# Graph attention's f column: 32-node blocks turned on VectorE and spread through DRAM instead of TensorE transposes

## The chip, the core and the metric

The kernel runs on one NeuronCore of a Trainium2 chip. The engines of a core work in parallel, each through its own list of instructions in order: TensorE (PE) does matmuls and transposes through the matmul array, VectorE (DVE) and ScalarE (ACT) do elementwise work, GpSimd (POOL) small side work, and SyncE (SP) issues the DMAs. PE writes into PSUM, which is eight banks here; everything else lives in SBUF, and inputs and outputs in DRAM. Engines wait for each other by semaphores. The metric is the device time of one launch in microseconds; the median of three runs before the change is 3039.1 us (3038.93 to 3040.48).

## What is computed

There are 64 graphs of 256 nodes with 256 features, and an adjacency matrix each. A graph passes four layers, each with a residual and a layer norm: multi-head attention with a feed-forward block, two graph attentions, and a relational convolution of two steps. The change concerns the two graph attentions. Cut to the core:

```python
Wh = einsum('bnd,de->bne', h, W)
f_i = Wh @ a1                                # one number per node
f_j = Wh @ a2
e = f_i[:, :, None] + f_j[:, None, :]        # 256 x 256 scores of a graph
e = leaky_relu(e, 0.2)
e = where(adj > 0, e, -inf)
alpha = softmax(e, axis=-1)
out = einsum('bij,bjd->bid', alpha, Wh)
```

The score of a pair of nodes is a sum of two numbers, one per node. In a tile with the key nodes on the partitions and the query nodes along the free dimension, one of the two (g) is a column that an instruction can add per partition; the other (f) must lie along the free dimension, the same row of 256 numbers on all 128 partitions. But the product that makes h leaves f as a column, one number per partition. Something has to turn it and spread it over the partitions.

## The kernel before

Graphs are handled one by one as sets of operations, and a planner in the kernel (`Plan`, lines 51 to 202) orders the operations of all 64 graphs together. Each operation has an engine, a cost in microseconds written beside it, the tiles that it reads and writes, and a due time that follows from the graph's number (46 us a graph). `schedule` plays the engines in time by these costs: each engine takes the ready operation with the earliest due time whose buffers are free. A result is seen by another engine a lag later (`LAG`, line 58; 3.5 us for SP), by the same engine at once (line 192). Buffers come from rings of fixed size (`RINGS`, line 25), eight PSUM banks among them. PE's three ways of tiling the array ("full", "row", "col") are kept together, and a change between them is given a cost (`SWITCH`). What comes out is one fixed order of instructions for each engine, including SP's DMAs; on the chip each engine follows its order and waits only for semaphores. At any time operations of about three graphs are mixed.

A graph attention is `gat` (lines 767 to 804). Its steps:

- the features are transposed on PE and evicted by ACT (`transposed`, L596 and L599);
- two products of 128 nodes each with the weights, widened by two columns for f and g (`product`, L605, "gw");
- eviction to the tile h, by ACT for layer 2 (L776), by DVE with a bias for layer 1 (L778);
- the spread of f: for each half of the nodes, one transpose on PE of the f column repeated over 128 columns. The result, f along the free dimension on every partition, is in a PSUM bank (L787);
- two score instructions on DVE, f + g, limited by the mask gm (L792), the leaky ReLU on DVE (L795), exp on ACT (L797);
- two products of e with h on PE (L605, "h,e"), which include the softmax sum through a column of ones, then reciprocal, scaling and residual on DVE, and the layer norm.

SP issues for each graph the loads of x, adj, xr (x once more) and adj again, each 256 KB, and the store of the result (L579, L902).

After the main path a check on sums decides whether a general, slow version is run as well; with these inputs it is not. It uses two constants, `eye` and `ones_b`, which are made at the kernel's start.

The lines around the change:

Of the kernel before, what the change touches and what calls it, by code (L numbers as in the profile page):

```python
# [25 lines left out]
         "xr": 2, "hid": 1, "h": 3, "e": 4, "n": 2, "rel": 3, "hi": 2, "lo": 2, "o": 4}  # L26
# [24 lines left out]
class Plan:  # L51
# [6 lines left out]
    LAG = {"PE": 0.21, "DVE": 0.13, "ACT": 0.13, "POOL": 0.08, "SP": 3.5}  # L58
    TO = {"PE": 0.06, "POOL": 0.05}
    SWITCH = 0.2  # L60
# [145 lines left out]
def tile_gnn_stack(ctx: ExitStack, tc: tile.TileContext, t: dict, out: bass.AP):  # L206
# [114 lines left out]
    ones_b = filled([P, P], BF16, "ones_b", 1.0)  # L321
    ones = filled([P, HD], F32, "ones", 1.0)
    neghalf = filled([P, NT], F32, "neghalf", -0.5)
    eye = filled([P, N // P, N], BF16, "eye", 0.0)
    for h in range(N // P):
        nc.vector.tensor_copy(eye[:, h, h * P : (h + 1) * P], ident_b)
# [153 lines left out]
    def main_path(plan):  # L480
# [11 lines left out]
        plan.ring("bank", 8, bank)  # L492

# [61 lines left out]
        def graph(g):  # L555
# [14 lines left out]

            def new(ring, shape, dtype=F32):
                return plan.tile(ring, shape, dtype)
# [16 lines left out]
            def transposed(xt):  # L589
# [9 lines left out]
                act(0.48, lambda: nc.scalar.copy(xT(), pt()), [pt], [xT])  # L599
# [7 lines left out]
            def layer_norm(y):  # L607
# [21 lines left out]
                dve(1.0, stats, [y], [mv, stat])  # L629
# [27 lines left out]
            def projections(xT):  # L657
# [22 lines left out]
                act(0.49, lambda: nc.scalar.copy(v(), pv()), [pv], [v])  # L680
                return qk, v

            def attention(xT, am):
# [6 lines left out]
                for kt in range(NB):  # L690
# [11 lines left out]
                    pe("row", 1.08, scores, [qk], s, [p[kt, r] for r in range(4)])  # L702
                    for r in range(4):
                        pr, k = p[kt, r], 8 * g + 4 * kt + r
                        act(0.61, lambda pr=pr, k=k, sr=s[r]: nc.scalar.activation(  # L705
# [8 lines left out]
                for hg in range(KB):  # L714
# [12 lines left out]
                    pe("col", 1.31, values, [v] + both + list(p.values()), [pc], [ctxT, inv])  # L727
                    dve(1.67, lambda hg=hg, pc=pc: nc.vector.reciprocal(inv()[:, hg, :], pc()[:, 1, :]), [pc], [(inv, hg)])  # L728
                    dve(0.34, lambda hg=hg, pc=pc: nc.vector.tensor_tensor(
                        ctxT()[:, hg, :], pc()[:, 0, :], inv()[:, hg, :], op=ALU.mult), [pc, (inv, hg)], [(ctxT, hg)])  # L730
                act(0.61, lambda: nc.scalar.activation(inv(), inv(), AF.Identity, accum_out=seen_inv[:, g : g + 1]), [inv], [inv])
                return ctxT

            def product_plus(lhs, reads, rhs, n, add):
# [5 lines left out]
                dve(0.66, lambda: nc.vector.tensor_tensor(y(), po(), add(), op=ALU.add), [po, add], [y])  # L740
# [26 lines left out]
            def gat(xt, layer, gm, seen, bias, finish):  # L767
# [3 lines left out]
                for i in range(NB):  # L771
# [3 lines left out]
                    if bias is None:  # L775
                        act(0.29, lambda i=i, ph=ph: nc.scalar.copy(h()[:, i, 0 : D + 2], ph()), [ph], [(h, i)])  # L776
                    else:
                        dve(0.34, lambda i=i, ph=ph: nc.vector.tensor_tensor(h()[:, i, 0 : D + 2], ph(), bias, op=ALU.add),  # L778
                            [ph], [(h, i)])
# [3 lines left out]
                pf = new("bank", [P, N])  # L783

                def spread():
                    for i in range(NB):
                        nc.tensor.transpose(pf()[:, i * P : (i + 1) * P],  # L787
                                            h()[:, i, F_COL : F_COL + 1].to_broadcast([P, P]), ident)

                pe("full", 0.22, spread, [(h, 0), (h, 1)], [pf], [e])  # L790
                for i in range(NB):
                    dve(0.40, lambda i=i: nc.vector.scalar_tensor_tensor(e()[:, i, :], pf(), h()[:, i, G_COL : G_COL + 1],  # L792
                                                                         gm()[:, i, :], op0=ALU.add, op1=ALU.min),
                        [pf, (h, i), gm], [(e, i)])
# [3 lines left out]
                for i in range(NB):  # L798
# [3 lines left out]
                    dve(0.12, lambda po=po, r=r: nc.vector.reciprocal(r(), po()[:, ONE : ONE + 1]), [po], [r])  # L802
# [13 lines left out]
            def layer2(xt, gm):  # L816
                def finish(i, z, po, r):
# [5 lines left out]
                    dve(0.37, lambda: nc.vector.scalar_tensor_tensor(n(), n(), 1.0, xt()[:, i, :], op0=ALU.min,  # L823
                                                                     op1=ALU.add), [n, xt], [n], "uses")
                    dve(0.37, lambda: nc.vector.scalar_tensor_tensor(zi(), n(), -1.0, zi(), op0=ALU.add, op1=ALU.max),
# [16 lines left out]
            def conv(h, layer, rel, rdeg):  # L842
# [18 lines left out]
                for j in range(NB):  # L861
# [8 lines left out]
                    pe("full", 0.46, gather, [rel, hi, lo], [pa])  # L870
# [288 lines left out]
```

## Time and profile before

| what | us |
|---|---|
| median of three runs | 3039.1 |
| time of the profiled execution | 3041.5 |
| its span, first to last instruction | 3039.6 |
| PE busy | 2949.0 (97%) |
| PE weight loads busy | 2257.9 (74%) |
| DVE busy | 2560.6 (84%) |
| ACT busy | 1574.8 (52%) |
| POOL busy | 761.8 (25%) |
| DMA queue of SP | 89.15 MB, 9.9% of 16 engines |

The span runs from the first to the last instruction of one profiled execution; its own time lies 1.9 us above the span and 2.4 us above the median. Busy time counts when an engine works on an instruction. Matmuls overlap, so the time that a matmul occupies PE is the distance to the next one's start and not its shown length. "Idle before" names how long an engine stood just before instructions of a group and what ended it. The mean granted clock of PE is 0.994 of full speed.

### The profile page before, as it was taken

The numbers are of one execution on the slowest core, as the hardware profiler recorded it, in microseconds if no ns is written. First come the engines' busy times: TensorE is split into PE (matmuls) and PEld (weight loads), VectorE is DVE, ScalarE is ACT, GpSimd is POOL, SyncE is SP. The second block draws the span as 40 slices with busy tenths as digits, with TensorE's granted clock in tenths as the row PEclk, the third lists the DMA queues.
The fourth block names the chain that finished last, engine by engine and source line by source line (L and its number), as shares of the span: only waits on it lengthen the run. The fifth ranks groups of instructions, "written<-read, shape, count | busy, mean of one in ns | idle before, by whom it ended". The sixth has DMA issues, their size and how long they took to land.

```text
span 3039.6 us, 49429 instructions
## 1 busy us (share of the span) xinstructions
PE 2949.0 (97%) x17462; PEld 2257.9 (74%) x17462; DVE 2560.6 (84%) x6368; ACT 1574.8 (52%) x3777; POOL 761.8 (25%) x1877
## 2 busy tenths in 40 slices
PE   8999999999999999999999999999999999999897
PEld 6777767777777777777777777777777777777584
DVE  6889798888797987988889888979889879897857
ACT  3455445555554554555455455545555545555444
POOL 2222222222222222222232222222222223222121
PEclk9999999999999999999999999999999999999999
DMA  5001011111010010010110101100101110001000
GB/s 155 25 22 36 19 34 32 29 28 32 22 32 29 29 36 28 25 32 28 29 32 25 36 22 32 32 29 28 30 27 29 29 31 29 28 25 29 8 11 15
DMA packets 91947, 93.56 MB, mean 31 GB/s; under 512 B 5648, under 2 KB 90896, under 8 KB 91696
## 3 DMA queue, kind: packets, MB, share of 16 engines
q1 hardware_dynamic: 91072, 89.15, 9.9%
q8 instruction: 141, 2.31, 0.3%
q0 software_dynamic: 624, 1.19, 0.2%
q14 instruction: 110, 0.90, 0.1%
HBM read 73.54 MB, written 16.78 MB: 30 GB/s over the span
## 4 chain that ended last, share of the span: by engine, by line
PE 71%; DVE 19%; ACT 4%; POOL 3%; issue 2%; SPq 1%; DMA 0%; POOLq 0%; ACTq 0%; DVEq 0%
PE bank L605 57%; PE bank L596 4%; PE bank L724 3%; PE bank L867 3%; DVE p L707 2%; PE bank L699 2%; PE bank L719 2%; DVE st L614 2%; ACT X L626 1%; POOL rstd L620 1%; ACT p L705 1%; DVE o L877 1%; DVE inv L728 1%; DVE both L711 1%; DVE X L740 1%
## 5 line engine op out<-in xcount | busy, mean ns | idle before, releaser
L619 POOL TENSOR_SCALAR rstd<-mv 128x2 f32<-128x2 f32 x384 | 134.0, 349 | 1535.2 <-DVE mv L616 1388.5
L605 PE MATMUL bank<-T,w 128*128 128x256 f32 x2048 | 480.7, 381 | 2.0 <-ACT T L599 1.4
L605 PE MATMUL bank<-cw,T 128*128 128x512 f32 x1024 | 469.7, 601 | 11.3 <-ACT T L599 8.8
L626 ACT ACTIVATE X<-X,rstd 128x256 f32<-128x256 f32 x640 | 349.8, 596 | 236.8 <-POOL rstd L622 151.2
L605 PE MATMUL bank<-w,hid 128*128 128x256 f32 x2048 | 463.3, 380 | 0.0
L605 PEld LDWEIGHTS bank<-w,hid 128*128 128x128 f32 x2048 | 383.5, 190 | 58.6 <-issue 5.1
L605 PEld LDWEIGHTS bank<-T,w 128*128 128x128 f32 x2048 | 376.6, 190 | 58.2 <-issue 5.1
L707 DVE TENSOR_TENSOR p<-p,am 128x512 f32<-128x512 f32 x512 | 329.0, 683 | 31.6 <-ACT p L705 30.2
L605 PEld LDWEIGHTS bank<-cw,T 128*128 128x128 f32 x1024 | 192.0, 192 | 212.6 <-issue 186.2
L705 ACT ACTIVATE p<-bank 128x512 f32<-128x512 f32 x512 | 300.7, 599 | 46.7 <-PE bank L699 45.9
L620 POOL TENSOR_TENSOR rstd<-rstd,neghalf 128x2 f32<-128x2 f32 x384 | 311.2, 810 | 32.0
L599 ACT COPY T<-bank 128x512 f32<-128x512 f32 x384 | 222.0, 586 | 184.8 <-PE bank L596 181.2
L605 PE MATMUL bank<-h,e 128*128 128x259 f32 x1024 | 251.3, 386 | 9.5 <-ACT e L797 7.1
L605 PE MATMUL bank<-T,wqkv 128*128 128x256 f32 x1024 | 247.4, 384 | 6.6 <-ACT T L599 6.6
L757 ACT ACTIVATE hid<-bank,col_b 128x256 f32<-128x256 f32 x512 | 212.1, 472 | 74.8 <-PE bank L605 72.7
L605 PE MATMUL bank<-gw,T 128*128 128x258 f32 x1024 | 247.1, 382 | 1.3 <-ACT T L599 1.2
L614 DVE BATCH_NORM_STATS2 st<-X 128x6 f32<-128x256 f32 x640 | 239.2, 416 | 5.1
L605 PEld LDWEIGHTS bank<-h,e 128*128 128x128 f32 x1024 | 190.7, 190 | 67.4 <-issue 28.0
L728 DVE RECIPROCAL inv<-bank 128x256 f32<-128x256 f32 x128 | 215.3, 1721 | 8.7 <-PE bank L724 8.7
L605 PEld LDWEIGHTS bank<-T,wqkv 128*128 128x128 f32 x1024 | 188.8, 191 | 37.4 <-ACT T L599 9.8
L605 PEld LDWEIGHTS bank<-gw,T 128*128 128x128 f32 x1024 | 190.0, 190 | 32.1 <-ACT T L599 3.2
L781 POOL TENSOR_TENSOR seen_fg<-h 128x4 f32<-128x4 f32 x128 | 54.8, 428 | 624.0 <-DVE h L778 322.7
(124 smaller groups left out, 4966.6 us busy)
## 6 DMA issues: line engine op xcount, KB each, us to landing
adj<-in_adj_dram SPq DMA_DIRECT2D x128, 256.0 KB, 2.8
x<-in_x_dram SPq DMA_DIRECT2D x64, 256.0 KB, 2.8
xr<-in_x_dram SPq DMA_DIRECT2D x64, 256.0 KB, 2.8
out_dram<-o SPq DMA_DIRECT2D x64, 256.0 KB, 2.1
w<-in_W1T_dram SPq DMA_DIRECT2D x1, 1024.0 KB, 12.2
w<-in_W2T_dram SPq DMA_DIRECT2D x1, 1024.0 KB, 19.0
wqkv<-in_WqkvT_dram SPq DMA_DIRECT2D x1, 768.0 KB, 4.7
cw<-in_w_root_dram SPq DMA_DIRECT2D x2, 256.0 KB, 5.5
```

The costliest lines, as they stand in the source:

```text
L596: nc.tensor.transpose(pt()[:, kb, i * P : (i + 1) * P], xt()[:, i, kb * P : (kb + 1) * P], ident)
L599: act(0.48, lambda: nc.scalar.copy(xT(), pt()), [pt], [xT])
L605: nc.tensor.matmul(dst, lhsT=lhs(c), rhs=rhs(c), start=(c == 0), stop=(c == n - 1))
L614: nc.vector.bn_stats(stat()[:, i, :], y()[:, i, :])
L619: nc.gpsimd.tensor_scalar(rstd()[:, 0, :], mv()[:, :, 1], 1.0, EPS, op0=ALU.mult, op1=ALU.add)
L620: nc.gpsimd.tensor_tensor(rstd()[:, 0, :], rstd()[:, 0, :], neghalf[:, 0:NB], op=ALU.pow)
L626: nc.scalar.activation(y()[:, i, :], y()[:, i, :], AF.Identity, bias=rstd()[:, 1, i : i + 1], scale=rstd()[:, 0, i : i + 1])
L705: act(0.61, lambda pr=pr, k=k, sr=s[r]: nc.scalar.activation(pr(), sr(), AF.Exp, accum_out=seen_sum[:, k : k + 1]), [s[r]], [pr])
L707: dve(0.60, lambda pr=pr, kt=kt: nc.vector.tensor_tensor(pr(), pr(), am()[:, kt, None, :].to_broadcast([P, KB, N]), op=ALU.mult), [pr, am] ...
L724: nc.tensor.matmul(pc()[32 * r : 32 * r + 32, 0, :], lhsT=v()[:, kt, HD * h : HD * (h + 1)], rhs=p[kt, r]()[:, hg, :], start=(kt == 0), st ...
L728: dve(1.67, lambda hg=hg, pc=pc: nc.vector.reciprocal(inv()[:, hg, :], pc()[:, 1, :]), [pc], [(inv, hg)])
L757: act(0.36, lambda f=f, k=k, ph=ph: nc.scalar.activation(hid()[:, f + k, :], ph()[:, k, :], AF.Relu, bias=b1[:, f + k : f + k + 1]), [ph, ...
```

## The change

The two PE transposes of each graph attention go. In their place DVE transposes f in blocks of 32 by 32: the f column, repeated 32 times, is turned so that the 32 partitions of a block each hold the block's 32 numbers. SP stores the four blocks of each half into a DRAM tile of 32 rows by 256, so that each of the 32 rows has all 256 numbers, and then loads the 32 rows four times over onto 128 partitions. The scores read f from SBUF instead of PSUM. New rings hold the turned blocks (`own`), the DRAM tile (`f_row`) and the loaded f (`f`), two of each.

`eye` and `ones_b` move into the general version. Some costs and lags that the planner reckons with are changed, so that it orders the work anew.

```diff
-    LAG = {"PE": 0.21, "DVE": 0.13, "ACT": 0.13, "POOL": 0.08, "SP": 3.5}
+    LAG = {"PE": 0.21, "DVE": 0.13, "ACT": 0.13, "POOL": 0.08, "SP": 3.2}
...
-    SWITCH = 0.2
+    SWITCH = 0.1
...
+            def sp(cost, issue, reads, writes):
+                op("SP", cost, issue, reads, writes)
...
-                pf = new("bank", [P, N])
-
-                def spread():
+                own, rows, pf = new("own", [P, NB * 32]), new("f_row", [32, N]), new("f", [P, N])
+
+                def turn():
                     for i in range(NB):
-                        nc.tensor.transpose(pf()[:, i * P : (i + 1) * P],
-                                            h()[:, i, F_COL : F_COL + 1].to_broadcast([P, P]), ident)
-
-                pe("full", 0.22, spread, [(h, 0), (h, 1)], [pf], [e])
+                        nc.vector.transpose(own()[:, i * 32 : (i + 1) * 32], h()[:, i, F_COL : F_COL + 1].to_broadcast([P, 32]))
+
+                dve(0.2, turn, [(h, 0), (h, 1)], [own], "uses")
                 for i in range(NB):
-                    dve(0.40, lambda i=i: nc.vector.scalar_tensor_tensor(e()[:, i, :], pf(), h()[:, i, G_COL : G_COL + 1],
-                                                                         gm()[:, i, :], op0=ALU.add, op1=ALU.min),
-                        [pf, (h, i), gm], [(e, i)])
+                    sp(0.42, lambda i=i: nc.sync.dma_start(rows()[:, i * P : (i + 1) * P].rearrange("r (b n) -> b r n", b=4),
+                                                           own()[:, i * 32 : (i + 1) * 32]), [own], [(rows, i)])
+                sp(0.42, lambda: nc.sync.dma_start(pf(), rows()[None, :, :].to_broadcast([4, 32, N])), [rows], [pf])
+                for i in range(NB):
+                    dve(0.35, lambda i=i: nc.vector.scalar_tensor_tensor(
+                        e()[:, i, :], pf(), h()[:, i, G_COL : G_COL + 1], gm()[:, i, :], op0=ALU.add, op1=ALU.min), [pf, (h, i), gm], [(e, i)], "uses")
...
-                    dve(0.12, lambda po=po, r=r: nc.vector.reciprocal(r(), po()[:, ONE : ONE + 1]), [po], [r])
+                    dve(0.08, lambda po=po, r=r: nc.vector.reciprocal(r(), po()[:, ONE : ONE + 1]), [po], [r])
```

About fifteen other cost figures change by a few hundredths up to 0.12, most of them downwards.

## The prediction

> **What bounds the kernel now.** I read the page's busy table first, then the busy time by stretch, then what TensorE (PE) waited for, then the timeline around the transposes, last the costs by group and the DMA lines.
>
> ```profile
> PE 2949.0 (97%) x17462; PEld 2257.9 (74%) x17462; DVE 2560.6 (84%) x6368; ACT 1574.8 (52%) x3777; POOL 761.8 (25%) x1877
> ```
>
> ```profile
> 1262.00:1540.00 278.00, 274.12 (x1637) 210.60 (x1634) 238.79 (x592) 146.27 (x352) 73.63 (x174) 1.00 0.10 28
> 1540.00:2800.00 1260.00, 1240.57 (x7352) 954.88 (x7352) 1082.72 (x2685) 667.27 (x1602) 329.10 (x792) 1.00 0.10 30
> 2800.00:2980.00 180.00, 162.81 (x929) 123.41 (x928) 132.36 (x332) 82.31 (x191) 33.98 (x110) 0.97 0.03 8
> 2980.00:3040.00 60.00, 41.92 (x162) 23.66 (x160) 42.26 (x132) 23.25 (x49) 9.61 (x31) 0.88 0.06 19
> ```
>
> After stretch and length come PE, PE's weight loads, DVE, ACT and POOL, then the granted clock. PE is busy 98.5% from 1262 to 2800 us and has holes only in the last 240 us, where three graphs drain. DVE, at 86%, is next. PE's waits, in total, times, longest:
>
> ```profile
> PE bank L605 <- ACT T L599: 18.0, 28, 1.1
> PE bank L596 <- ACT X L626: 8.6, 23, 1.7
> PE bank L605 <- ACT e L797: 7.1, 10, 2.4
> PE bank L787 <- DVE h L778: 1.5, 4, 0.8
> ```
>
> The list adds up to some 75 us, start and end included. So the kernel is bound by PE's instruction stream, and a wait put into that stream is paid in full. The attention scores e cost PE only 7.1 us of waiting. The timeline of one spread:
>
> ```profile
> 1288.20 1.03 PE L605 MATMUL bank<-T,w 128*128 128x256 f32 x4
> 1289.06 0.38 PE L787 MATMUL bank<-ident,h 128*128 128x128 f32 x2
> 1289.28 3.60 PE L605 MATMUL bank<-cw,T 128*128 128x512 f32 x8
> 1292.72 0.60 PE L605 MATMUL bank<-h,e 128*128 128x259 f32 x2
> ```
>
> From 1289.06 to the next start, 1289.28, the two transposes hold PE for 0.22 us, although each is shown 0.27 long: matmuls overlap. Costs and transfers (the DMA column is issue to landing):
>
> ```profile
> L787 PE MATMUL bank<-ident,h 128*128 128x128 f32 x256 | 50.6, 276 | 3.4 <-ACT p L705 1.8 <-DVE h L778 1.5
> L792 DVE SCALAR_TENSOR_TENSOR e<-bank,h,gm 128x256 f32<-128x256 f32 x256 | 111.4, 473 | 29.2 <-PE bank L787 29.2
> L823 DVE SCALAR_TENSOR_TENSOR n<-n,X 128x256 f32<-128x256 f32 x128 | 50.3, 414 | 0.0
> L652 DVE TENSOR_TENSOR am<-am,ident_b 128x128 bf16<-128x128 bf16 x128 | 22.9, 221 | 1.6
> L802 DVE RECIPROCAL r<-bank 128x1 f32<-128x1 f32 x256 | 38.7, 157 | 22.5 <-PE bank L605 22.0
> ```
>
> ```profile
> adj<-in_adj_dram SPq DMA_DIRECT2D x128, 256.0 KB, 2.8
> ...
> out_dram<-o SPq DMA_DIRECT2D x64, 256.0 KB, 2.1
> ```
>
> ```profile
> q1 hardware_dynamic: 91072, 89.15, 9.9%
> ```
>
> ```profile
> 1273.42 0.37 SPq L579 DMA_DIRECT2D x<-in_x_dram  x1
> ```
>
> One packet on queue 1 takes 0.099 x 16 x 3039.6 / 91072 = 0.053 us; an issue holds SP 0.37 us.
>
> **The change, part by part.** There are 64 graphs with two graph attentions each: 128 spreads.
>
> *Removed from PE.* 256 transposes, by the spacing above 128 x 0.22 = 28.2 us. The busy column's 50.6 is the far bound. I take 28.2, because the next matmul already starts after 0.22. As PE is the bound, this comes off the end, unless something new stops PE.
>
> [...]
>
> *DVE.* It gains 256 transposes of 32 columns: between L802 (157 ns, one column) and L652 (221 ns, 128 columns), nearer the former, say 170: +44 us. The 256 score instructions read f from SBUF instead of PSUM: 473 to 414 (L823, the same operation from SBUF), -15 us. DVE goes to about 2590 us, 85%; PE's 98% still covers that. If DVE's idle time (16%) were used up, each of these 29 us would show.
>
> *Planner's numbers, ones_b and eye.* The order is replanned. Changes of PE's tiling mode in it go from 345 to 352; each costs about 0.09 (0.31 instead of 0.22 before a row or column stretch), so under 1 us. The constants' memsets move out of the start: under 1 us, beside DMAs. The ops' cost figures change no instruction.
>
> *The path of f.* Formerly evict h, 0.22 us of PE, scores. Now: evict h, two transposes, two stores of 16 KB, a wait on SP for both to land, one load of 128 KB, scores. SP's issues rise from 354 to 738: 384 x 0.37 = 142 us, on an engine otherwise idle; but SP is in order, so while it waits for the stores to land (some 2 us, 128 times) the loads and stores of other graphs queue behind it; they have tens of us. In 123 of 128 cases load follows stores directly; in 91 a load of x, xr or adj stands directly before the stores, and if its buffer comes free late, f is late.
>
> Call X the time from the end of the transposes to f being usable. Handovers are 0.1 each. With 256 KB over 16 engines (16 packets each, 0.85 us), a store has 2.1 - 0.85 = 1.25 us without packets and a load 2.8 - 0.85 = 1.95. The trace has no DMA of this shape; the old ones have 128 rows outermost, the new ones' DRAM side has a dimension of 4 outermost.
> - Low end, all 16 engines: stores 0.37 + 1.25 + 8 x 0.053 = 2.0; load 1.95 + 0.42 = 2.4; X = 0.1 + 2.0 + 2.4 + 0.1 = 4.6.
> - High end, four engines, and a 128-byte packet as dear as a 1 KB one: stores 1.25 + 64 x 0.053 = 4.6; load 1.95 + 32 x 0.053 = 3.65; X = 8.5.
> - Taken: four engines, on the assumption that a DMA is cut along its outermost dimension, which is 128 in the old ones and four here; 128-byte packets at 0.015, nearer their share by bytes (0.007) than the full price: stores 1.25 + 64 x 0.015 = 2.2, load 3.65: X = 6.05.
>
> [...]
>
> The planner's own idea is shorter: its code adds SP's lag of 3.2 to other engines only (line 192), so it lets the load issue as soon as the stores are issued: 0.13 + 3 x 0.42 + 3.2 = 4.6 us. It fills just that much. Where X is longer, PE arrives at the product early and stands.
>
> How much stands there? From the last matmul that makes h (L605, gw) to the product with e (L605, h,e) the chain now takes 0.16 (result after its 0.22 spacing) + 0.37 (eviction) + 0.3 (transposes) + X + 0.86 + 0.69 + 0.63 (scores, leaky ReLU, exp, durations of L792, L795, L797) + four handovers 0.4 = 3.4 + X. Against it I put the PE work that lies between the two in the changed order, at the old spacing: 0.433 per 256-column product, 0.86 per 512, 0.11 per transpose, 0.135 per score matmul, 0.11 per column-tiled one. One case: 16 products with hid (6.93) and 4 with ctxT (1.73) make 8.66. The deciles of the 128 windows are 7.8, 8.2, 8.6, 9.0, 9.2, 10.0, 10.2, 10.8, 11.8; in the last eight only 3.9 to 6.6. In the order of before the median is 6.5 and the chain 3.6 (its part from h to the scores is 0.58 by the timeline); this account then gives 2 us of standing, and the profile 7.1. Adding up what the chain exceeds its window by, with windows that overlap counted once:
> chain 8.0: 13 us; 8.6: 27; 9.0: 43; 9.4: 64; 10.0: 101; 11.8: 255. About 15 of the 64 fall in the last eight windows.
>
> With X = 6.05 the chain is 9.4: +64 us. While PE stands, ACT and DVE catch up: of the 45 us or so that PE waits for others between start and end, I take off a quarter, 12.
>
> **Sum**, against the profiled execution (span 3039.6, its time 3041.5, which is 2.4 above the median 3039.1): 3041.5 - 28 + 64 - 12 = 3065; on the median's scale 3063.
>
> **Rivals.**
> 1. *The transfers are quick and hidden: faster.* X = 4.6, chain 8.0: 3041.5 - 28 + 13 - 2.4 = 3024. For it: the planner reckons with this X, and loads of 256 KB land in 2.8. Against: the DRAM side in blocks of 32 by four, and a store that must land first. It decides below X = 5.2 (chain 8.6, 27 us: break-even).
> 2. *DVE, held at the scores, becomes the bound.* DVE is in order; between transposes and scores its new order has 4.6 us of work in the mean. At X = 6 it is held 198 us in all, in 104 of 128 cases. Of its 479 idle us that would leave 250, but what queues behind the scores (masking p, sums for layer norms) then reaches PE late as well. If half of the 198 reaches PE in place of the 64: 3041.5 - 28 + 99 - 2.4 = 3110. For it: 86% busy between 60 and 2800. Against: such lateness mostly falls into the same standing of PE.
> 3. *Gain and standing cancel*: X about 5.2 to 5.4, 3034 to 3045.
>
> **Chances.** Forecast (chain 9.0 to 10: 3041 to 3100) 0.43; rival 1 (3015 to 3032) 0.34; rival 2 (3090 to 3140) 0.15; rival 3 0.08. A measurement of this kernel tells about 0.2%, 6 us, from no change. So faster 0.34, same 0.08, slower 0.58. Range 3019 to 3118: it cuts the fast end of rival 1 and the slow end of rival 2; the high end X = 8.5 (chain 11.9, some 3270) stays out as unlikely. The likeliest case's own range is 3041 to 3100.
>
> **What will show it.** Right: the loads of f land 3.4 to 3.8 us after issue and the stores about 2; PE's wait for e (ACT, L803) rises from 7 to 50 us or more, in some 60 cases; DVE waits for f at L799; PE's busy time falls by 28 us or, by the column, up to 50. Wrong: f landing in about 2.4 and PE's wait for e under 20 us, then the time is near 3024; or DVE's wait at L799 over 150 us with PE standing for T, X and p too, then over 3090. Also wrong if PE's own order has become worse elsewhere, which waits for others than e would tell.

## The result and the profile after

The changed kernel takes 3222.51 us (median of four, 3220.49 to 3228.47) against 3039.79 (3038.93 to 3040.92) for the kernel before: a ratio of 1.0604 with a 95% interval of 1.0586 to 1.0622. It is 183 us slower. The forecast was 3063 with a range of 3019 to 3118: the direction was right, the size was not. The profiled execution took 3220.49, its span is 3218.7, and its mean granted clock is 0.981 (0.994 before).

Busy time and the chain of waits of the changed kernel (the chain's first line by engine, its second by line):

```profile
PE 2993.2 (93%) x17206; PEld 2260.7 (70%) x17206; DVE 2588.0 (80%) x6620; ACT 1577.3 (49%) x3777; POOL 712.6 (22%) x1877
PE 42%; DVE 32%; DMA 16%; issue 4%; ACT 3%; POOL 2%; SPq 0%; POOLq 0%; DVEq 0%; ACTq 0%
PE bank L607 34%; DMA f<-f_row 11%; DMA f_row<-own 5%; DVE p L709 4%; DVE st L616 2%; DVE e L799 2%; PE bank L598 2%; DVE inv L730 2%; DVE o L883 2%; PE bank L726 2%; DVE e L801 2%; PE bank L873 2%; DVE mv L618 1%; DVE X L585 1%; DVE both L713 1%
```

Before, the chain was 71% PE and 0% DMA. Now the two steps through DRAM, the load of f and the stores, are 16% of it, and DVE is 32%. PE has 256 instructions fewer and yet shows 44 us more busy time, a point that comes back below.

The run in stretches, first one row of the kernel before, then the changed kernel (stretch, length, then PE, its weight loads, DVE, ACT, POOL, the granted clock):

```profile
60.00:1262.00 1202.00, 1184.14 (x7089) 907.68 (x7087) 1026.19 (x2542) 634.90 (x1531) 303.28 (x745) 1.00 0.10 29
```

```profile
60.00:1262.00 1202.00, 1139.89 (x6604) 863.38 (x6604) 990.72 (x2533) 608.26 (x1459) 266.09 (x712) 0.99 0.12 34
1262.00:1540.00 278.00, 254.95 (x1459) 192.13 (x1457) 214.84 (x548) 132.78 (x313) 61.19 (x164) 0.97 0.11 32
1540.00:2980.00 1440.00, 1353.64 (x7837) 1022.84 (x7837) 1177.19 (x3008) 716.35 (x1725) 327.67 (x840) 0.99 0.12 34
```

From 60 to 1262 us PE did 7089 matmuls and now does 6604; from 1262 to 1540 us it was busy 274 of 278 us and did 1637, now it is busy 255 and does 1459. The loss is spread over the whole run and is not an effect of the end.

Waits of PE, and below them of DVE (total, times, longest):

```profile
PE bank L607 <- ACT e L803: 54.0, 34, 3.3
PE bank L607 <- issue: 42.7, 34, 3.2
PE bank L598 <- ACT X L628: 31.1, 46, 5.4
PE bank L607 <- ACT T L601: 17.1, 26, 2.8
PE bank L873 <- DVE lo L861: 15.5, 18, 2.6
```

```profile
DVE e L799 <- DMA f<-f_row: 243.6, 116, 6.6
DVE X L742 <- PE bank L607: 129.1, 59, 6.2
DVE lo L861 <- ACT hi L860: 55.8, 53, 4.9
```

PE's wait for e, where the profile names e, is 54.0 us (7.1 before) in 34 cases, close to the 50 us that the forecast gave as its sign. The 42.7 us of "issue", where the profile names no releaser, stand before the same products of h with e. All idle time of PE before these products, in the changed kernel:

```profile
L607 PE MATMUL bank<-h,e 128*128 128x259 f32 x1024 | 275.6, 414 | 108.6 <-ACT e L803 54.0 <-issue 42.7 <-ACT T L601 2.8
```

So PE stands 108.6 us there (9.5 before). And DVE stands 243.6 us for f, and PE also waits longer for X (31.1 us, 8.6 before) and lo (15.5, 2.9 before), though not for T (17.1, 18.0 before). That is for the most part the sign that the prediction gave for its rival 2: DVE held over 150 us, with PE standing for other results too.

One spread in the timeline:

```profile
1515.10 0.30 DVE L791 STREAM_TRANSPOSE own<-h 128x32 f32<-128x32 f32 x2
...
1515.33 1.08 SPq L795 DMA_DIRECT2D f_row<-own  x2
...
1517.87 0.54 SPq L797 DMA_DIRECT2D f<-f_row  x1
...
1522.05 0.91 DVE L799 SCALAR_TENSOR_TENSOR e<-f,h,gm 128x256 f32<-128x256 f32 x2 [0.32 <-DMA f<-f_row]
```

The transposes end at 1515.40, the scores begin at 1522.05, released by the load: X is 6.65 us. Read in this way over all 128 spreads, the median is 6.65 and the mean 6.8 (0.6 from store to store, 2.0 from the second store to the load, 4.06 from the load to the scores).

And what it costs, first DVE, then PE in the same place:

```profile
2417.36 0.33 DVE L791 STREAM_TRANSPOSE own<-h 128x32 f32<-128x32 f32 x2
...
2423.11 0.88 DVE L799 SCALAR_TENSOR_TENSOR e<-f,h,gm 128x256 f32<-128x256 f32 x2 [3.83 <-DMA f<-f_row]
2424.02 0.69 DVE L801 SCALAR_TENSOR_TENSOR e<-e 128x512 f32<-128x512 f32 x1
2428.24 0.88 DVE L799 SCALAR_TENSOR_TENSOR e<-f,h,gm 128x256 f32<-128x256 f32 x2 [3.53 <-DMA f<-f_row]
...
2429.77 0.69 DVE L585 TENSOR_TENSOR X<-X,row_ln_g 128x512 f32<-128x512 f32 x1
```

```profile
2425.48 1.99 PE L607 MATMUL bank<-h,e 128*128 128x259 f32 x8 [1.13 <-issue]
2430.62 3.23 PE L607 MATMUL bank<-h,e 128*128 128x259 f32 x8 [3.15 <-issue]
```

DVE stands 3.8 us for one f and, three instructions later, 3.5 us for the next one; the layer norm's work of L585 and all behind it begin only after both. The second f was turned by 2417.69 and is usable at 2428.24, 10.6 us later: its stores left SP only at 2419.94, because SP stood with the first spread's load until 2419.30.

### The profile page after: what moved, and what is told of

Its sections match the earlier page's. It is cut to its first block, busy times and chain, and to the rows that moved or that the text cites. A ratio compares the mean times of both kernels' runs of the same rounds, so it can differ in the third digit from the quotient of the medians.

```text
span 3218.7 us, 49919 instructions
## 1 busy us (share of the span) xinstructions
PE 2993.2 (93%) x17206; PEld 2260.7 (70%) x17206; DVE 2588.0 (80%) x6620; ACT 1577.3 (49%) x3777; POOL 712.6 (22%) x1877
## 4 chain that ended last, share of the span: by engine, by line
PE 42%; DVE 32%; DMA 16%; issue 4%; ACT 3%; POOL 2%; SPq 0%; POOLq 0%; DVEq 0%; ACTq 0%
PE bank L607 34%; DMA f<-f_row 11%; DMA f_row<-own 5%; DVE p L709 4%; DVE st L616 2%; DVE e L799 2%; PE bank L598 2%; DVE inv L730 2%; DVE o L883 2%; PE bank L726 2%; DVE e L801 2%; PE bank L873 2%; DVE mv L618 1%; DVE X L585 1%; DVE both L713 1%
## 5 line engine op out<-in xcount | busy, mean ns | idle before, releaser
L621 POOL TENSOR_SCALAR rstd<-mv 128x2 f32<-128x2 f32 x384 | 121.6, 317 | 1965.3 <-DVE mv L618 1666.6
L607 PEld LDWEIGHTS bank<-T,w 128*128 128x128 f32 x2048 | 385.0, 192 | 64.7 <-ACT T L601 5.7
L607 PE MATMUL bank<-h,e 128*128 128x259 f32 x1024 | 275.6, 414 | 108.6 <-ACT e L803 54.0
L607 PEld LDWEIGHTS bank<-h,e 128*128 128x128 f32 x1024 | 199.3, 203 | 179.7 <-issue 142.8
L799 DVE SCALAR_TENSOR_TENSOR e<-f,h,gm 128x256 f32<-128x256 f32 x256 | 113.3, 481 | 243.9 <-DMA f<-f_row 243.6
L803 ACT ACTIVATE e<-e 128x512 f32<-128x512 f32 x128 | 80.6, 630 | 297.1 <-DVE e L801 291.3
```

What stands on the lines that cost most here:

```text
L607: nc.tensor.matmul(dst, lhsT=lhs(c), rhs=rhs(c), start=(c == 0), stop=(c == n - 1))
L621: nc.gpsimd.tensor_scalar(rstd()[:, 0, :], mv()[:, :, 1], 1.0, EPS, op0=ALU.mult, op1=ALU.add)
L799: dve(0.35, lambda i=i: nc.vector.scalar_tensor_tensor(e()[:, i, :], pf(), h()[:, i, G_COL : G_COL + 1], gm()[:, i, :], op0=ALU.add, op1=A ...
L803: act(0.52, lambda: nc.scalar.activation(e(), e(), AF.Exp), [e], [e])
```

## The experiments

Times are medians with their lowest and highest. Each experiment is compared with the kernel before on the same chip; the ratio has its 95% interval.

**Which part of the change costs? e1: the changed kernel with PE's spread back.**

```diff
-                own, rows, pf = new("own", [P, NB * 32]), new("f_row", [32, N]), new("f", [P, N])
+                pf = new("bank", [P, N])
...
-                dve(0.2, turn, [(h, 0), (h, 1)], [own], "uses")
+                pe("full", 0.22, spread, [(h, 0), (h, 1)], [pf], [e])
...
-                sp(0.42, lambda: nc.sync.dma_start(pf(), rows()[None, :, :].to_broadcast([4, 32, N])), [rows], [pf])
```

> The changed kernel with the spread of f put back on PE (two transposes into a PSUM bank, scores from the bank); the new cost figures, lags, SWITCH and the moved constants stay. Theory A (the path of f through DRAM costs all the time, the replanned order nothing): within 0.5% of before, 3025 to 3055 us. Rival (the new cost figures give a worse order): 3100 us or more, and then at least 60 of the 183 us belong to them.

Measured: 3045.94 (3042.58 to 3047.56) against 3042.17, ratio 1.0013 (1.0003 to 1.0022). The planner's new figures, the moved constants and the order made from them cost 4 us. The other 179 belong to the change from PE's spread to the path of f.

**e2: the changed kernel with no spread at all; the scores read a constant row.**

```diff
-                own, rows, pf = new("own", [P, NB * 32]), new("f_row", [32, N]), new("f", [P, N])
+                pf = c_f
...
-                dve(0.2, turn, [(h, 0), (h, 1)], [own], "uses")
...
-                sp(0.42, lambda: nc.sync.dma_start(pf(), rows()[None, :, :].to_broadcast([4, 32, N])), [rows], [pf])
```

> The changed kernel without the path of f: no transposes, no stores, no loads; the scores read a constant zero tile in its place, so f is left out of the scores. Theory A (removing 128 pairs of PE transposes is worth their spacing, 0.22 us each): 3039 - 28 = 3011, between 3000 and 3022. Rival (the pairs are worth the busy column, 50 us, or more because a PSUM bank per attention comes free): under 3000. If it is over 3030, the gain was never there.

Measured: 3040.18 (3038.86 to 3043.83) against 3042.17, ratio 0.9995 (0.9986 to 1.0005). Both theories missed; it is the third outcome that was named, over 3030: with the transposes gone and nothing in their place, 6 us are gained against e1, not 28. The removal was therefore tested by itself below (e7, e8, e11, e12).

**e3: PE's spread is used, and the new chain runs beside it unread.**

```diff
-                sp(0.42, lambda: nc.sync.dma_start(pf(), rows()[None, :, :].to_broadcast([4, 32, N])), [rows], [pf])
+                sp(0.42, lambda: nc.sync.dma_start(spare(), rows()[None, :, :].to_broadcast([4, 32, N])), [rows], [spare])
...
+                pe("full", 0.22, spread, [(h, 0), (h, 1)], [pf], [e])
```

> The changed kernel with both: PE spreads f as before and the scores use that; besides, f is turned on DVE, stored and loaded as in the change, and nobody reads it. Theory A (it is the wait for f that costs): 3040 to 3075, since DVE has 51 us more of transposes and SP more to issue but nothing waits. Rival (contention: DVE's extra work, SP's queue held by its waits, DMA traffic): 3130 or more.

Measured: 3049.26 (3046.65 to 3049.99), ratio 1.0023 (1.0013 to 1.0033), 3 us above e1. The 384 DMAs, their packets and DVE's 256 transposes cost almost nothing as work, so contention is not what costs. What is left is the wait for f; e13 takes it away by itself.

**e4: the planner is told what the path takes, X = 6.9 us: 0.6 per store, 1.5 from the stores to the load, 0.55 for the load, 3.5 until it has landed.**

```diff
-    LAG = {"PE": 0.21, "DVE": 0.13, "ACT": 0.13, "POOL": 0.08, "SP": 3.2}
+    LAG = {"PE": 0.21, "DVE": 0.13, "ACT": 0.13, "POOL": 0.08, "SP": 3.5}
+    STORE = 1.5
...
-                    a.ready = max(a.ready, end if a.engine == e else seen + self.TO.get(a.engine, 0.0))
+                    a.ready = max(a.ready, (end + self.STORE if e == "SP" else end) if a.engine == e
+                                  else seen + self.TO.get(a.engine, 0.0))
...
-                    sp(0.42, lambda i=i: nc.sync.dma_start(rows()[:, i * P : (i + 1) * P].rearrange("r (b n) -> b r n", b=4),
+                    sp(0.6, lambda i=i: nc.sync.dma_start(rows()[:, i * P : (i + 1) * P].rearrange("r (b n) -> b r n", b=4),
...
-                sp(0.42, lambda: nc.sync.dma_start(pf(), rows()[None, :, :].to_broadcast([4, 32, N])), [rows], [pf])
+                sp(0.55, lambda: nc.sync.dma_start(pf(), rows()[None, :, :].to_broadcast([4, 32, N])), [rows], [pf])
```

> The changed kernel with the planner told what the trace of the changed kernel shows: a load of f may issue 1.5 us after the stores' issue ends (before: at once), issues cost 0.6 and 0.55, SP's lag 3.5. The median PE work between h and its product with e grows from 9.2 to 11.9 us, DVE's work between transposes and scores from 4.6 to 6.6 us in the mean. Theory A (the path is 2.2 us longer than the planner thought and each engine stands for that): with a chain of 10.2 the account of windows gives 26 us of standing instead of 116; time 3020 to 3070, PE's clock back to 0.99. Rival (the path itself, two DMAs in a row on an in-order SP, is what costs, however it is planned): over 3130.

Measured: 3056.05 (3054.33 to 3061.87), ratio 1.0052 (1.0035 to 1.0068). The same instructions in an order that knows the delay: 166 of the 183 us are back. The path itself had not become shorter: from the first store to the load are 2.6 us as in the changed kernel. X, read up to the scores, is 7.4 us in the median, but DVE stands for f in only 31 of the 128 cases, and in the others X includes time in which f was there and DVE was at other work. DVE's and PE's waits in e4:

```profile
DVE e L801 <- DMA f<-f_row: 49.6, 31, 6.6
```

```profile
PE bank L600 <- ACT X L630: 15.5, 27, 4.6
PE bank L609 <- ACT T L603: 14.7, 22, 2.2
PE bank L609 <- ACT e L805: 9.7, 11, 3.4
```

DVE is held 49.6 us instead of 243.6, PE waits 9.7 for e.

**e5: the planner's figures as in the changed kernel, but quicker DMAs: stores of four rows, and a load with 128 outermost on both sides.**

```diff
-                own, rows, pf = new("own", [P, NB * 32]), new("f_row", [32, N]), new("f", [P, N])
+                own, rows, pf = new("own", [P, NB * 32]), new("f_row", [1, N]), new("f", [P, N])
...
-                    sp(0.42, lambda i=i: nc.sync.dma_start(rows()[:, i * P : (i + 1) * P].rearrange("r (b n) -> b r n", b=4),
-                                                           own()[:, i * 32 : (i + 1) * 32]), [own], [(rows, i)])
-                sp(0.42, lambda: nc.sync.dma_start(pf(), rows()[None, :, :].to_broadcast([4, 32, N])), [rows], [pf])
+                    sp(0.42, lambda i=i: nc.sync.dma_start(rows()[0:1, i * P : (i + 1) * P].rearrange("r (b n) -> (r b) n", b=4),
+                                                           own()[0:P:32, i * 32 : (i + 1) * 32]), [own], [(rows, i)])
+                sp(0.42, lambda: nc.sync.dma_start(pf(), rows()[0:1, :].to_broadcast([P, N])), [rows], [pf])
```

> The changed kernel in its own order, instruction for instruction; only the DMAs' shape is changed: each store writes 4 rows of 32 numbers (one partition of each block) instead of 128, the load reads one row 128 times, so that 128 is outermost. Theory A (what counts is by how much the path of f exceeds the 4.6 us that the planner reckons with): the load lands in about 2.5 instead of 3.6 us, the path falls from 6.7 to about 5.3; the account of windows gives 30 to 45 us of standing instead of 116, time 3070 to 3120. Rival (the stores' round trip and SP's queue are the cost, the shape is not): 3180 or more.

Measured: 3072.76 (3071.03 to 3074.47) against 3040.49, ratio 1.0103 (1.0086 to 1.012). Median X is 5.25 (the load 3.18 instead of 4.06), DVE is held 103.7 us, PE waits 18.4 for e. With 1.3 us less of X (mean) and the same order on every engine, 150 of the 183 us are gone.

**e6: the planner is told half of it, X = 5.8.** The rest is as in e4.

```diff
-    LAG = {"PE": 0.21, "DVE": 0.13, "ACT": 0.13, "POOL": 0.08, "SP": 3.2}
+    LAG = {"PE": 0.21, "DVE": 0.13, "ACT": 0.13, "POOL": 0.08, "SP": 3.3}
+    STORE = 0.6
```

> As the run with the corrected planner, but corrected by half: a load of f may issue 0.6 us after its stores' issue, SP's lag 3.3, so that the planner reckons with 5.8 us for the path. The chip's path stays at 6.7 us. Windows: median 10.8 us. Theory A: between the changed kernel and the corrected one; the account gives 39 us of standing at a chain of 10.2 (116 and 26 there), so 3080 to 3110. Rival (what helped was something else in the new order, or any longer lag is as good): within 10 us of 3056.

Measured: 3079.16 (3076.95 to 3082.51), ratio 1.013 (1.0113 to 1.0147); DVE held 90.5 us, PE 17.2 for e. It lies between the changed kernel and e4, about as expected.

**What is the removal worth? e7: the kernel before without its spread, the scores reading a constant. e8: the kernel before with the spread done twice.**

```diff
-                pf = new("bank", [P, N])
...
-                pe("full", 0.22, spread, [(h, 0), (h, 1)], [pf], [e])
+                pf = c_f
```

```diff
-                    for i in range(NB):
+                    for i in [*range(NB), *range(NB)]:
...
-                pe("full", 0.22, spread, [(h, 0), (h, 1)], [pf], [e])
+                pe("full", 0.44, spread, [(h, 0), (h, 1)], [pf], [e])
```

> The kernel before, with its old cost figures, without any spread of f: the scores read a constant zero tile, so f is left out of the scores. Theory B (the freed PE time is lost again because in this order PE waits for other engines' results, whatever the figures): 3030 to 3045, as in the run with the new figures. Rival (the new cost figures ate the gain of 28 us): 3005 to 3018.

> The kernel before with the spread done twice on PE, the second time over the first (256 transposes more, nothing else). If PE's stream is the bound and a pair is worth its spacing: 3039 + 28 = 3067. If the pairs lie in time that PE does not need (Theory B taken to its end): under 3050.

Measured: e7 3031.12 (3027.28 to 3031.45) against 3040.49, ratio 0.9967 (0.9954 to 0.9979), 9 us less; e8 3087.11 (3085.64 to 3088.7), ratio 1.0151 (1.0134 to 1.0168), 47 us more. So 256 transposes less and 256 more are not mirror images, and neither is the spacing's 28; for e8 neither of the two expected outcomes came. Each kernel here has an order of its own, planned anew.

**e11 and e12: the same removal in orders with slack. Both are the kernel before with longer lags in the plan, so that results come early; e12 has the first edit alone, e11 both.**

```diff
-    LAG = {"PE": 0.21, "DVE": 0.13, "ACT": 0.13, "POOL": 0.08, "SP": 3.5}
+    LAG = {"PE": 0.31, "DVE": 0.33, "ACT": 0.33, "POOL": 0.28, "SP": 3.5}
```

```diff
-                pe("full", 0.22, spread, [(h, 0), (h, 1)], [pf], [e])
+                pf = c_f
```

> The kernel before without any spread (f left out of the scores, a zero tile in its place), old figures, with the planner's lags 0.1 to 0.2 us longer. Theory B: the missing 19 of the 28 us come back, 3008 to 3020. Rival (another engine, DVE at 86%, bounds this kernel from below): 3025 to 3040.

> The kernel before, with the spread on PE, with the planner's lags 0.1 to 0.2 us longer: the control to the run without a spread. Theory B: it gains less, 3025 to 3040, and the difference of the two is nearer 28 than 9 us. Rival: unchanged or slower, and the difference stays under 15.

Measured: e11 3022.95 (3020.85 to 3025.17) against 3040.59, ratio 0.9941 (0.9926 to 0.9956); e12 3049.57 (3047.26 to 3050.29), ratio 1.0027 (1.0017 to 1.0038). Between the two lie 26.6 us, near the spacing's 28, as Theory B had it; but neither came to its own expected time, e11 missed by 3 us and e12 by 10, and against the kernel before e11 gains only 18. That PE saves the spacing's 28 when others' results are ready in time fits this pair and is not shown by it. Why e12 is slower than the kernel before, whose lags are shorter, was not looked into; orders planned with slightly different figures differ by several us for no reason that these runs show.

**A version that beats both? e9: one store for both halves, e5's load, and a planner told X = 5.0. e10: the same, told 5.6 and with the lags of e12.** Both have e4's line for `STORE`; e9's figures are 1.1 for it and 2.9 for SP's lag, e10's are shown.

```diff
-    LAG = {"PE": 0.21, "DVE": 0.13, "ACT": 0.13, "POOL": 0.08, "SP": 3.2}
+    LAG = {"PE": 0.31, "DVE": 0.33, "ACT": 0.33, "POOL": 0.28, "SP": 3.1}
+    STORE = 1.3
...
-                for i in range(NB):
-                    sp(0.42, lambda i=i: nc.sync.dma_start(rows()[:, i * P : (i + 1) * P].rearrange("r (b n) -> b r n", b=4),
-                                                           own()[:, i * 32 : (i + 1) * 32]), [own], [(rows, i)])
-                sp(0.42, lambda: nc.sync.dma_start(pf(), rows()[None, :, :].to_broadcast([4, 32, N])), [rows], [pf])
+                sp(0.55, lambda: nc.sync.dma_start(rows()[0:1, :].rearrange("r (i b n) -> (r b) i n", i=NB, b=4),
+                                                   own()[0:P:32, :].rearrange("p (i n) -> p i n", i=NB)), [own], [rows])
+                sp(0.35, lambda: nc.sync.dma_start(pf(), rows()[0:1, :].to_broadcast([P, N])), [rows], [pf])
```

> f's path made short and reckoned with: one store of 4 rows instead of two (both halves in one DMA), a load with 128 outermost, and a planner that knows that the load waits (1.1 us after the store's issue) and lands in 3.25: 5.0 us in all. Theory A: the path on the chip is about 4.8 (0.6 less than with two short stores), it fits what was planned, PE's wait for e goes to 10 us or less; the time is that of the kernels without a spread, 3025 to 3045. Rival (any path through DRAM costs, since SP's and DVE's queues are in order): 3055 or more.

> The same with all the planner's lags 0.1 to 0.2 us longer, so that each result is reckoned later than it comes. Theory B (PE stands in small pieces because the planner's windows are tight to 0.1 us): 10 to 20 us below the run with one store. Rival (longer windows hold more graphs' buffers, nothing is won): the same within 6 us or slower.

Measured: e9 3039.74 (3036.18 to 3046.18) against 3040.59, ratio 0.9998 (0.9989 to 1.0007): no difference. e10 3027.64 (3024.94 to 3028.18), ratio 0.9954 (0.994 to 0.9967): 13 us faster than the kernel before, 22 faster than e12 with the same lags, and within 5 of e11, which has no spread at all. Busy time, chain and DVE's wait of e10:

```profile
PE 2935.9 (97%) x17206; PEld 2244.2 (74%) x17206; DVE 2584.8 (85%) x6620; ACT 1573.2 (52%) x3777; POOL 729.1 (24%) x1877
PE 75%; DVE 18%; ACT 3%; issue 2%; POOL 1%; DMA 1%; SPq 0%; POOLq 0%; DVEq 0%; ACTq 0%
```

```profile
DVE e L800 <- DMA f<-f_row: 43.9, 30, 4.7
```

DMA is 1% of the chain, and PE is the bound again. f still goes through DRAM.

**Whose wait is it? e13 and e14 keep the changed kernel's order on every engine and take one dependence away. e13: the chain runs, but the scores read a constant row, so DVE does not stand for f. e14: the scores wait for f, but PE's products read a constant instead of e.**

```diff
-                        e()[:, i, :], pf(), h()[:, i, G_COL : G_COL + 1], gm()[:, i, :], op0=ALU.add, op1=ALU.min), [pf, (h, i), gm], [(e, i)], "uses")
+                        e()[:, i, :], conv_b[0], h()[:, i, G_COL : G_COL + 1], gm()[:, i, :], op0=ALU.add, op1=ALU.min), [pf, (h, i), gm], [(e, i)], "uses")
```

```diff
-                    pe("full", 0.87, lambda i=i, po=po: product(po(), lambda kt: e()[:, kt, i * P : (i + 1) * P],
+                    pe("full", 0.87, lambda i=i, po=po: product(po(), lambda kt: ln1g[:, i * P : (i + 1) * P],
```

> The changed kernel, every engine's order unchanged, all transposes, stores and loads of f still made, but the scores read a constant row (the bias row of the first convolution) instead of f, so that nobody waits for f; f is left out of the scores. It shows what this order costs when f is never late. If lateness of f is all that is wrong: 3030 to 3050. Rival (this order, planned with wrong figures, or its DMA traffic costs by itself): 3080 or more.

> The changed kernel, every engine's order unchanged, the scores wait for f as in the change, but the products with h read a constant (the row of ln1's gain) in place of e, so that PE never waits for e; the attention weights are left out. DVE is still held at the scores. If PE's own wait for e is the cost: within 15 us of the run in which f is unread. If DVE's being held reaches PE through its other results: 60 us or more above it. Half and half (60 to 110 us above it) if the two share the 180 us.

Measured: e13 3038.12 (3034.59 to 3039.0) against 3041.62, ratio 0.9989 (0.9979 to 0.9998); e14 3192.69 (3184.34 to 3205.38), ratio 1.0498 (1.0464 to 1.0533). Without the stand for f the changed order is as quick as the old one, with all its DMAs and transposes: nothing of the loss against the kernel before is in the order or in the work (the 28 us that the removal was to gain are missing all the same). With the stand for f, but with PE never waiting for e, 155 us of loss remain. PE's and DVE's waits of e14:

```profile
PE bank L598 <- ACT X L628: 62.6, 80, 11.0
PE bank L873 <- DVE lo L861: 25.6, 37, 2.4
PE bank L607 <- ACT T L601: 24.8, 30, 3.9
PE bank L598 <- DVE o L889: 9.3, 16, 1.4
```

```profile
DVE e L799 <- DMA f<-f_row: 241.5, 119, 6.4
DVE X L742 <- PE bank L607: 125.2, 59, 6.2
```

In e13 the first of these is 24.6 us. PE now stands for X, lo and T: results that have nothing to do with f, except that DVE makes them, or the sums they need, behind the scores. The last 30 us or so, from 3193 to 3222, come back with PE's own wait for e.

## Why the prediction was wrong

**The step that failed is the standing, +64 − 12.** It measured the chain from h to the product with e against PE's work between the two, and charged PE only for the product that comes too early, less a quarter for other waits. The measure is e13: the same instructions in the same order on PE, DVE not standing for f. The changed kernel's profiled span is 181.5 us longer, 3218.7 against 3037.2. Busy times and the row of the product in e13:

```profile
PE 2941.2 (97%) x17206; PEld 2242.8 (74%) x17206; DVE 2578.8 (85%) x6620; ACT 1576.4 (52%) x3777; POOL 730.9 (24%) x1877
L607 PE MATMUL bank<-h,e 128*128 128x259 f32 x1024 | 255.4, 393 | 12.4 <-issue 6.9 <-ACT e L803 4.0 <-POOL rstd L623 0.5
```

- Before the product with e PE stands 108.6 us instead of 12.4: +96, where the prediction has +64. This part of the account was sound and was fed a short X: with the chain of 10.2 that the measured X gives, it yields 116 (the figure in the expectation of e4).
- Before all its other instructions PE stands 33 us more, where the prediction takes 12 off because "ACT and DVE catch up". DVE is itself the engine that is held.
- The same instructions take 52 us more of PE's busy time, a term that the prediction does not have; it comes back under the clock.

With 116 for 64 the prediction's own sum is 3115. The other 107 us lie in the last two points and in the removal (below). Nor is the place of a stand its price. e14 takes PE's wait before the product away, and 155 of the 185 us between e13 and the changed kernel remain: PE stands elsewhere instead. So DVE's stand alone is enough for most of the loss. The 30 that remain are what the product's wait adds behind DVE's stand; a run with that wait alone was not made, so 155 and 30 are not shares of two separate causes.

Rival 2 described this, but said that "such lateness mostly falls into the same standing of PE" and counted half of it. As to the place that is right, 96 of the 129 us of added standing; as to the price it is not, for with the place gone the price stays. Rival 2 was also held down by its size: the stand was put at 198 us for X = 6 and was 243.6, and of that 184, three quarters, came through. Its 3110 was 112 us short, and the range, which ended at 3118, left such a time out.

What a stand costs can be read from the kernels that differ in it. For each: X in the planner's figures, X measured (mean, up to the scores), DVE's stand for f, and the median less that of the kernel before on its chip. DVE stands for f in 116 of the 128 cases in the changed kernel, in 61 and 73 in e5 and e6, and in some 30 in e4, e9 and e10. Where it does not, it comes later than f, and X holds its own delay too; so the mean is an upper bound, most of all in the last three.

| kernel | X planned | X measured | stand | loss |
|---|---|---|---|---|
| changed | 4.6 | 6.8 | 243.6 | +182.7 |
| e5 | 4.6 | 5.55 | 103.7 | +32.3 |
| e6 | 5.8 | 7.05 | 90.5 | +38.7 |
| e4 | 6.9 | 7.7 | 49.6 | +13.9 |
| e9 | 5.0 | 5.6 | 45.0 | −0.9 |
| e10 | 5.6 | 5.8 | 43.9 | −13.0 |

The changed kernel, e5 and e13 have one and the same order on every engine: there the first 103.7 us of standing cost 36 us (e5 against e13), the next 139.9 cost 150. So the first part of the stand was paid by a third and the second in full. e9 and e10 stand some 45 us and lose nothing; that DVE, 84% busy before, has that much to give is a guess, since these two have other orders and the removal's gain besides. The loss follows neither X alone (e4's is the longest) nor DVE's share of busy time (80% to 85% in all of them), but goes in the order of the amount by which X exceeds what the plan allowed: 2.2, 0.95, 1.25, 0.8, 0.6 and 0.2 us in the order of the table. A planner that fills just its own X, as the prediction said this one does, leaves nothing for the error.

**X, 6.05: the runs agree with the mechanism, the size was a little low.** Measured 6.65 in the median and 6.8 in the mean. The stores took 2.6 instead of 2.2: the second one issues 0.6 after the first, a term that the sum for 6.05 leaves out, though the one for 4.6 has it with 0.37. The load took 4.06 to the scores instead of 3.65 + 0.1. By the prediction's own table these 0.6 to 0.75 us are worth some 40 to 50 us of standing. Four engines, the assumption on which X rested, agree with a count, though no trace names the engine of a packet. DMA queue 1, which had 91072 packets before, in the changed kernel and in e5:

```profile
q1 hardware_dynamic: 141760, 110.13, 12.0%
```

```profile
q1 hardware_dynamic: 111552, 106.07, 11.6%
```

The changed kernel has 50688 packets more, 396 for each of 128 spreads: 2 x 128 rows of 128 bytes, 128 rows of 1 KB, and 12 over. In the trace those 12 are packets of four bytes that close the three DMAs, four each; a load of 256 KB closes with 16. In 43 loads of f that had the DMAs to themselves 3.7 packets of 1 KB were under way in the mean and at most 7; in 72 such loads of 256 KB, 10.7 and at most 22. In e5 it is 160 for each: 2 x 4 rows, 128 rows, and 24 over, which fits 4 + 4 for the stores, as in the changed kernel, and 16 for the load with 128 outermost. That load was usable 0.9 us sooner. The low end of X, 16 engines and 4.6 us, and with it rival 1's 3024, are excluded for this kernel. The high end's dear 128-byte packets, with 4.6 us for the stores, are excluded as well.

SP's order was priced for other graphs' loads only. In the place shown above it delayed the next spread by SP's stand with a load, so that X was 10.6; in 10 of the 128 cases the first store left more than 0.1 us after the transposes had ended.

**The removal, −28.2: right as PE's own time, wrong as a gain.** It is worth 26.6 us between the two orders with slack (e11 against e12), 9 in the kernel before (e7), 6 in the changed one (e2 against e1), and 3.5 in the changed kernel's order (e13 against before). "As PE is the bound, this comes off the end" did not hold. In the profiles PE's idle time, span less busy, grows by 16 us from e1 to e2 and by 5 from before to e7, but by 1 from e12 to e11, while its busy time falls by 20, 17 and 25. So in e2 the saved time becomes waiting, and in e7 the busy column itself falls by less than 28. Each pair compares two orders planned anew, so a difference of a few us need not be the removal's.

**The sum, term by term**, predicted −28, +64, −12, which is +24. Shown by the runs, each step on one chip or between the two medians: −3.5 (e13 against before), +155 (e14 against e13), +30 (changed against e14). The first term missed by 25 us, the others by 133; together they are, within 3 us, the 159 between 3063 and 3222 (the kernel before is 1.8 us slower on the chip of e13 and e14).

**DVE's busy time, +29: right in the sum by luck, wrong in both parts.** It rose by 27.4 us. The groups:

```profile
L791 DVE STREAM_TRANSPOSE own<-h 128x32 f32<-128x32 f32 x256 | 42.3, 198 | 15.8 <-ACT h L778 15.5
L799 DVE SCALAR_TENSOR_TENSOR e<-f,h,gm 128x256 f32<-128x256 f32 x256 | 113.3, 481 | 243.9 <-DMA f<-f_row 243.6
```

A transpose is 198 ns and not 170, and the scores are not quicker from SBUF: 481 ns against 473 from PSUM, where 414 was expected; the 414 was that of an instruction with three f32 operands, and the scores' mask gm is bf16 (that this is the cause no run shows). By the busy column the transposes add 42.3 and the scores 1.9; what takes 17 us off again was not followed. That this work has no effect on the end held (e3, e13).

**The planner's numbers, under 1 us**: e1 shows 4, with an interval that begins at 1; nothing of the 183.

**PE's clock was not in the prediction at all.** Its mean went from 0.994 to 0.981, and PE's busy time rose though it had less to do. In some of the places where it stands, the clock drops. One of them (changed kernel; PE's timeline, then stretches of 3.4 us):

```profile
2230.97 3.60 PE L607 MATMUL bank<-cw,T 128*128 128x512 f32 x8
2236.93 3.31 PE L607 MATMUL bank<-h,e 128*128 128x259 f32 x7 [2.37 <-ACT e L803]
```

```profile
2229.20:2232.60 3.40, 3.40 (x14) 2.32 (x13) 0.26 (x1) 3.00 (x8) 0.00 (x0) 1.00 0.39 84
2232.60:2236.00 3.40, 1.96 (x5) 0.57 (x3) 1.45 (x3) 0.00 (x0) 0.00 (x0) 1.00 0.42 109
2236.00:2239.40 3.40, 2.47 (x6) 2.02 (x7) 1.87 (x7) 1.17 (x3) 0.00 (x0) 0.60 0.02 5
2239.40:2242.80 3.40, 3.40 (x20) 3.00 (x19) 2.42 (x10) 0.00 (x0) 0.00 (x0) 0.90 0.00 0
```

After a gap of 2.37 us the granted clock is 0.60 in the next stretch, and seven of the products' matmuls with e take 3.31 us, where eight took 1.99 at 2425.48. Stretches that are laid 0.65 us later show it whole, 0.50 behind one of 1.00 in which PE was busy for 1.31 us:

```profile
2233.25:2236.66 3.41, 1.31 (x4) 0.24 (x2) 1.57 (x3) 0.50 (x1) 0.00 (x0) 1.00 0.20 52
2236.66:2240.08 3.42, 3.15 (x8) 2.52 (x9) 2.07 (x6) 0.66 (x3) 0.00 (x0) 0.50 0.02 5
```

Not each stand does this: from 1449.90 to 1452.51 PE stood 2.61 us for lo, was busy 0.80 us of the 3.40 from 1449.10, and the clock stayed at 1.00 in the next two stretches of 3.40. Where the clock drops, a stand is paid twice. An estimate of the second payment, from the mean clocks: (1 − 0.981) x 3218.7 = 61 us of lost clock against (1 − 0.992) x 3037.2 = 24 in e13, 37 us at most, since some of it falls into stretches where PE waits anyway. In the busy column the same instructions take 52 us more than in e13 (2993.2 against 2941.2). The clock explains at most its 37 of these; what the rest is was not looked into, and how much of the 184 the clock costs was not separated by a run.

## What to carry to other kernels

When an engine that works in order is made to wait, price the wait by everything that queues behind it and by who needs that, not only by the consumer of the late result: here three quarters of DVE's stand came through, and in one and the same order the last 140 us of it were paid in full. When a plan sets the order, tell it the measured delay of a new path, including a DMA that must land before the next one on the same queue can go; here that alone gave back 166 of 183 us. Work taken from the bound engine need not pay its spacing: here 28 us of it paid between 3.5 and 26.6, the most where the plan had slack, so try taking away work and loosening the plan together (e10).

## What the runs showed of the hardware

- The stores and loads of f in the changed kernel, with four outermost on the DRAM side, closed with four packets of four bytes each, the loads of 256 KB with 16. Their issue held SP longer: 0.51 us for a store and 0.545 for a load of f, against 0.37 for a load of 256 KB and 0.34 for e5's load with 128 outermost (at 1527.31).
- A store to DRAM followed by a load of the same data on one queue took, from the end of the transposes to the scores, 6.65 us in the changed kernel, 5.25 in e5 and 5.4 in e9 (medians). In the 31 cases of e9 in which DVE stood for f it was 4.84; in the others DVE came later than f. From one store's issue to the issue of the load that waits for it were 1.6 us with 4 to 8 packets of data, 2.0 with 128.
- PE's granted clock halved after gaps of 2.37 us (shown above) and of 3.15 us (0.51 from 2431.27 to 2434.69), each time behind a stretch of 3.41 us in which PE had also worked, 1.31 and 0.65 us; after one of 2.61 us (1449.90 to 1452.51) it stayed at 1.00.
- A transpose of 32 columns on DVE took 198 ns; a scalar_tensor_tensor of 256 columns took 481 ns from SBUF and 473 from PSUM with a bf16 third operand, while the same operation of L829, without one, took 416.
